# Projections, content products and output products on four column tiles of 32 in a fused attention and gate kernel

## The chip, the cores and the metric

The kernel runs on one core of one Trainium2 chip. The metric is the device time of one execution in microseconds (us). Engine names as in the profile: PE is TensorE (matmuls), PEld its weight loads, DVE is VectorE, ACT is ScalarE, POOL is GpSimd, SP is SyncE, which issues the DMAs.

## The reference

The input `x` has 8 batches of 256 rows of 512 values. It is normalized, goes through a latent attention with 128 heads and through a feed-forward branch, and the two are multiplied and added to `x`. Everything is float32.

```python
xn = layernorm(x)                                            # 8 x 256 x 512
c_q, c_kv = xn @ Wq_down, xn @ Wkv_down                      # latents of 64
q_c = (c_q @ Wq_up).reshape(b, s, 128, 4)                    # content part of the queries
q_r = (xn @ Wq_rope).reshape(b, s, 128, 64)                  # the large projection: 512 x 8192
k_c = (c_kv @ Wk_up).reshape(b, s, 128, 4)
v_c = (c_kv @ Wv_up).reshape(b, s, 128, 4)
k_r = xn @ Wk_rope                                           # one for all heads
scores = (q_c . k_c + q_r . k_r) / sqrt(68)                  # per head, 256 x 256
out = (softmax(scores) @ v_c).reshape(b, s, 512) @ Wo
g = silu(ffn(xn))
result = x + out * g
```

## The kernel before

A first phase of about 260 us normalizes `x`, transposes it, computes the latents and the gate `g` of all rows, and leaves them in DRAM. Its matmuls have their own lines (L364 to L471). The attention follows, in 64 blocks of 16 heads of one batch: `blocks` goes over pairs of batches, within a pair over eight groups of heads, and within a group over the two batches. There is no scheduler: the order of instructions on each engine is the order in the code.

A block has two halves. In each half the loop issues, for TensorE, in this order:

1. `score` twice (tiles `sc`, L613): the content part from `qcm` and `kc`, then two parts from `qr` and `act`. These matmuls use 32 rows of the array each, four beside one another ("32*128" in the profile). They write four banks of PSUM.
2. one `Project` (tiles `q`, L162): a quarter of the large projection of a pair of batches, in seven products by Strassen's scheme, each over two chunks of 128 rows, 256 columns wide. That is 14 matmuls. `first` issues eight of them into four banks, ScalarE takes the four banks out (`take`, L202), `second` issues six more. There are 128 projections; four are made in the first phase and 124 in the main loop, two to a block in the first 62 blocks.
3. in the first half of a block only: every second block the content products `qk` of a coming group (`prepare`, L234 and L235), then the value products `av` of the block before (`weigh`, L657), 64 matmuls with 32 columns of weights, on four column tiles of the array ("128*32"). Block 0 has no `weigh`. After some blocks `values` follows (L261), also on column tiles.
4. in the second half of some blocks: the output products `po` of 128 rows (`finish`, L702), four matmuls with 512 columns.

Meanwhile VectorE finds the maxima of the scores (L626) and transposes the exponentials (L642), ScalarE makes the exponentials (L632) and takes the banks out, GpSimd joins the projection's sums (L207 to L209) and spreads the queries (L246). The weights of the next projections (`w`, `ws`) come by DMA from SP's queue; the sums of `x` (`xs`) come once for each pair of batches, four times in all, into a single buffer.

All banks of PSUM come from one pool of eight (`bank`), each of 128 partitions by 512 values. The matmuls of L162, L234, L235 and L702 fill all 128 partitions of their part of a bank in one instruction ("128*128"); those of L657 fill 32 partitions each:

```python
for k in range(8):
    for r in range(4):
        nc.tensor.matmul(
            av[32 * r : 32 * r + 32, ds(half * P, P)],
            vpad[:, k, r, :],
            pt[r][:, k].rearrange("p q i -> p (q i)"),
```

The functions that the diff touches, and what calls them:

Of the kernel before, what the change touches and what calls it, by code (L numbers as in the profile page):

```python
# [15 lines left out]
P = 128  # L16
B, S, D = 8, 256, 512
NT = B * S
KT = D // P
# [14 lines left out]
def mla_ffn_gate_kernel(  # L34
# [19 lines left out]
    nc = tc.nc  # L54
# [8 lines left out]
    wupq_sb = const.tile([P, 4, P], F32, name="wupq_sb")  # L63
    wupk_sb = const.tile([P, 4, P], F32, name="wupk_sb")
# [30 lines left out]
    def bank(name):  # L95
        return ps_all.tile([P, 512], F32, tag="b", name=name)
# [4 lines left out]
    acts, qks, qcms, valls, vpad_of, qrs = {}, {}, {}, {}, {}, {}  # L101
# [52 lines left out]
    def load_xs(p):  # L154
        if p < B // 2:
            xsums[p] = xsp.tile([P, 7, 2, S], F32, tag="xs", name=f"xs_{p}")
            nc.sync.dma_start(out=xsums[p], in_=xs_d[p])

    def product(bank_, w, x, first):

        for c in range(2):
            nc.tensor.matmul(  # L162
                bank_,
                w[:, c],
                x[:, c],
                start=first and c == 0,
                stop=c == 1,
                skip_group_check=True,
            )

    class Project:

# [20 lines left out]
        def first(self):  # L193

            for i, (w, x) in enumerate(
                ((self.a(0, 0), 0), (self.s[:, 1], 4), (self.s[:, 2], 5), (self.s[:, 0], 3))
            ):
                self.banks.append(bank(f"q{i}_{self.j}")[:, 0:S])
                product(self.banks[i], w, self.x[:, x], True)
# [11 lines left out]
        def second(self):  # L211

            for i, w, x in ((0, self.a(0, 1), 1), (2, self.a(1, 1), 6), (3, self.s[:, 3], 2)):
                product(self.banks[i], w, self.x[:, x], False)
            nc.scalar.copy(self.out(0, 0), self.split(self.banks[0]))
# [14 lines left out]
    def prepare(b, g):  # L230


        qk = bank(f"qk_{b}_{g}")
        nc.tensor.matmul(qk[:, :S], wupq_sb[:, g, :], acts[b][:, 0, :], start=True, stop=True)  # L234
        nc.tensor.matmul(qk[:, S:], wupk_sb[:, g, :], acts[b][:, 0, :], start=True, stop=True)  # L235
        qc = qcp.tile([P, S], F32, tag="qc", name=f"qc_{b}_{g}", bufs=3)
        nc.scalar.copy(qc, qk[:, :S])  # L237
        kc = qcp.tile([P, S], F32, tag="kc", name=f"kc_{b}_{g}", bufs=3)
        nc.scalar.mul(kc, qk[:, S:], QSCALE)
        qks[b, g] = qc, kc  # L240
# [307 lines left out]
    def between(step):  # L548
        if step == 0:
            set_up()  # L550
        elif step == 1:
            load_act(0)
            load_act(1)
            for j in range(2):
                load_rope(j)
        elif step == 2:
            prepare(0, 0)
            prepare(1, 0)
            spread(0)
            values(0)  # L560
            values(1)
            place_values(0)
            sum_w(0)
            sum_w(1)
            load_xs(0)
        elif step == 3:
            for j in range(2):
                Project(j).all()
                load_rope(j + 2)
                sum_w(j + 2)  # L570
        else:
            for j in range(2, 4):
                Project(j).all()
                load_rope(j + 2)
                sum_w(j + 2)
            load_act(2)
            load_act(3)
# [5 lines left out]
    wo_sb = w2p.tile([P, KT, D], F32, name="wo_sb")  # L583
# [11 lines left out]
    scs, nmxs, prs, pts, accs, outT = {}, {}, {}, {}, {}, {}  # L595
# [102 lines left out]
    def finish(b, n):  # L698
        g, xr = gxs.pop((b, n))
        po = bank(f"po_{b}_{n}")  # L700
        for c in range(KT):
            nc.tensor.matmul(  # L702
                po, outT[b][:, c, ds(n * P, P)], wo_sb[:, c, :], start=(c == 0), stop=(c == KT - 1)
            )
        nc.vector.tensor_mul(g, po, g)
        nc.gpsimd.tensor_add(g, g, xr)
        nc.sync.dma_start(out=out[ds(b * S + n * P, P), :], in_=g)
# [6 lines left out]
    for n, (b, sg) in enumerate(blocks):  # L714
        for half in range(2):
# [39 lines left out]
            if half == 0:  # L755
                if n + 2 <= last and blocks[n + 2][1] % 2 == 0:
                    prepare(blocks[n + 2][0], blocks[n + 2][1] // 2)
                if n < last:
                    spread(n + 1)
                if n >= 2 and blocks[n - 2][1] % 2:  # L760
                    normalize(n - 2)
                if n >= 1:
                    weigh(n - 1)
                    place_values(n)
                if (sg == 7 and b % 2) or (sg == 0 and b and b % 2 == 0):
                    if b + 1 < B:
                        values(b + 1)
                if sg == 2 and b >= 2:
                    load_act(b + 2)
            elif n in outs:  # L770
                finish(*outs[n])
    normalize(last - 1)
    load_out(B - 2, 0)
    finish(B - 2, 0)
    load_out(B - 2, 1)
    finish(B - 2, 1)
    load_out(B - 1, 0)
    weigh(last)
# [70 lines left out]
```

## Time and profile before

| what | value |
|---|---|
| median of 3 runs | 2095.45 us (2091.44 to 2098.23) |
| the profiled execution, its own time | 2094.74 us |
| its span | 2093.0 us |
| granted TensorE clock, mean | 0.992 |
| TensorE busy | 2046.5 us (98%) |
| VectorE, ScalarE, GpSimd busy | 1525.3, 1085.1, 719.2 us |
| records of matmuls, and of weight loads | 25536 each |

The span is the time from the first to the last instruction of the profiled execution. Busy time is the time in which at least one instruction of an engine is recorded as running. A record of a matmul has a start that is measured and an end that is modelled, and matmuls overlap, so that the busy time of TensorE and the mean of one instruction say little; the distance of two starts says what one costs. "128*32" stands for the rows and the columns of the array that an instruction uses, "128x256" for partitions by columns of what is streamed through it.

### The profile page before, as it was taken

What the parts mean: (1) busy time and instruction counts of PE and PEld (TensorE: products, weight loads), DVE (VectorE), ACT (ScalarE), POOL (GpSimd) and SP (SyncE); (2) the same over time, 40 slices, a digit from 0 to 9 for tenths busy, and PEclk for the clock granted to TensorE, in tenths of its full rate; (3) what the DMA queues carried; (4) which work ended last, traced back from release to release, by engine and by line L of the source; (5) the groups of instructions that cost most, each with busy time, mean ns of one, the idle gap of its engine ahead of it and who ended that gap; (6) DMA issues with size and microseconds to landing.
All of it is one profiled execution on the core that took longest, in us unless ns stands there. A gap on an engine that the chain in (4) does not pass through costs nothing.

```text
span 2093.0 us, 61071 instructions
## 1 busy us (share of the span) xinstructions
PE 2046.5 (98%) x25536; PEld 1671.2 (80%) x25536; DVE 1525.3 (73%) x2601; ACT 1085.1 (52%) x2989; POOL 719.2 (34%) x1037
## 2 busy tenths in 40 slices
PE   7999999999999999999999999999999999999996
PEld 3334688888888888888888888888888888888883
DVE  5332177878887777878786877788886867788895
ACT  2222265555655555555655545455555544565562
POOL 5335434555452322333233223332223233232321
PEclk9999999999999999999999999999999999999998
DMA  4233322222223132322123222222231232222201
GB/s 161 83 109 117 102 87 82 82 81 73 73 89 121 63 106 84 110 82 78 66 83 118 76 98 94 95 82 82 69 111 68 87 107 87 75 70 82 82 32 52
DMA packets 110262, 183.13 MB, mean 87 GB/s; under 512 B 8154, under 2 KB 80474, under 8 KB 108964
## 3 DMA queue, kind: packets, MB, share of 16 engines
q1 hardware_dynamic: 109988, 179.23, 24.6%
q8 instruction: 203, 3.33, 0.6%
q14 instruction: 71, 0.58, 0.1%
HBM read 145.12 MB, written 34.08 MB: 86 GB/s over the span
## 4 chain that ended last, share of the span: by engine, by line
PE 94%; DVE 2%; DMA 2%; POOL 1%; issue 0%; SPq 0%; ACT 0%; POOLq 0%; ACTq 0%; DVEq 0%
PE q L162 38%; PE sc L613 31%; PE av L657 11%; PE po L702 2%; PE px L428 2%; PE py L429 2%; PE pf L471 1%; PE px L414 1%; DMA xs<-xs_d 1%; DVE pt L642 1%; DVE nmx L626 1%; PE pm L381 1%; PE vps L261 1%; PE qk L234 1%; PE qk L235 1%; PE pp L381 1%
## 5 line engine op out<-in xcount | busy, mean ns | idle before, releaser
L632 ACT ACTIVATE pr<-sc,nmx 128x256 f32<-128x256 f32 x2048 | 818.7, 504 | 488.4 <-DVE nmx L626 486.9
L626 DVE TENSOR_REDUCE nmx<-sc 128x2 f32<-128x512 f32 x1024 | 635.6, 683 | 343.3 <-PE sc L613 311.9
L642 DVE STREAM_TRANSPOSE pt<-pr 128x512 f32<-128x512 f32 x1024 | 635.0, 678 | 0.0
L613 PE MATMUL sc<-act,qr 32*128 32x256 f32 x8192 | 493.8, 375 | 0.2 <-issue 0.2
L162 PE MATMUL q<-xs,ws 128*128 128x256 f32 x2048 | 486.7, 381 | 0.0
L207 POOL TENSOR_TENSOR e<-e,e 128x256 f32<-128x256 f32 x128 | 93.2, 728 | 1089.1 <-ACT e L202 568.9
L613 PEld LDWEIGHTS sc<-act,qr 32*128 32x128 f32 x8192 | 425.1, 185 | 23.1 <-issue 1.0
L162 PEld LDWEIGHTS q<-xs,ws 128*128 128x128 f32 x2048 | 391.4, 191 | 52.5 <-issue 0.2
L162 PE MATMUL q<-xs,w 128*128 128x256 f32 x1536 | 389.7, 390 | 10.3 <-DMA xs<-xs_d 7.5
L162 PEld LDWEIGHTS q<-xs,w 128*128 128x128 f32 x1536 | 292.3, 197 | 80.1 <-ACT pr L632 44.3
L613 PE MATMUL sc<-kc,qcm 32*128 32x256 f32 x4096 | 287.5, 388 | 2.6 <-ACT gs L475 2.5
L613 PEld LDWEIGHTS sc<-kc,qcm 32*128 32x128 f32 x4096 | 201.7, 185 | 53.1 <-issue 22.1
L657 PE MATMUL av<-pt,vpad 128*32 128x128 f32 x8192 | 236.8, 273 | 1.2 <-ACT pr L632 1.2
L657 PEld LDWEIGHTS av<-pt,vpad 128*32 128x32 f32 x8192 | 219.7, 110 | 22.9 <-POOL e L208 8.0
L202 ACT COPY e<-q 128x256 f32<-128x256 f32 x512 | 204.2, 400 | 29.4 <-PE q L162 20.8
L670 ACT ACTIVATE acc<-av,sides_sb 128x256 f32<-128x256 f32 x128 | 53.9, 472 | 242.3 <-PE av L657 242.3
L246 POOL TENSOR_TENSOR qcm<-qc,mask_sb 128x1024 f32<-128x1024 f32 x64 | 122.4, 1912 | 17.0 <-ACT qc L237 17.0
L432 DVE TENSOR_TENSOR hT<-gate,py 128x512 f32<-128x512 f32 (+1 forms) x48 | 32.5, 685 | 110.0 <-PE py L429 109.9
L209 POOL TENSOR_TENSOR qr<-e,e 128x256 f32<-128x256 f32 x128 | 93.8, 732 | 10.0
L208 POOL TENSOR_TENSOR e<-e,e 128x256 f32<-128x256 f32 x128 | 93.5, 730 | 10.0
L219 DVE TENSOR_TENSOR qr<-e,q 128x256 f32<-128x256 f32 x128 | 54.0, 422 | 44.5 <-POOL e L207 34.0
L276 POOL COPY vpad<-vall 32x128 f32<-32x128 f32 x256 | 76.8, 300 | 13.8 <-PE av L657 4.7
(94 smaller groups left out, 1125.4 us busy)
## 6 DMA issues: line engine op xcount, KB each, us to landing
w<-in_w_rope_dram SPq DMA_DIRECT2D x128, 512.0 KB
ws<-sums_d SPq DMA_DIRECT2D x96, 512.0 KB
sums_d<-ws SPq DMA_DIRECT2D x32, 512.0 KB
xs<-xs_d SPq DMA_DIRECT2D x4, 1792.0 KB
xt<-in_x_dram SPq DMA_DIRECT2D x16, 256.0 KB
xs_d<-xt SPq DMA_DIRECT2D x4, 1024.0 KB
gate_d<-gs SPq DMA_DIRECT2D x16, 256.0 KB
g<-gate_d SPq DMA_DIRECT2D x16, 256.0 KB
```

The costliest lines, as they stand in the source:

```text
L162: nc.tensor.matmul(bank_, w[:, c], x[:, c], start=first and c == 0, stop=c == 1, skip_group_check=True,)
L202: nc.scalar.copy(self.e[i], self.banks[i])
L207: nc.gpsimd.tensor_add(m6, m6, m1)
L208: nc.gpsimd.tensor_add(m7, m7, m6)
L209: nc.gpsimd.tensor_add(self.out(1, 1), self.split(m7), self.split(m5))
L246: nc.gpsimd.tensor_mul(qcm, qks[b, sg // 2][0].rearrange("p (q i) -> p q i", i=32).unsqueeze(2).to_broadcast([P, 8, 4, 32]), mask_sb[:, ds ...
L276: nc.gpsimd.tensor_copy(vpad[rows, :, :, 8 * t + 4 * (sg % 2) :][..., :4], valls[b][rows, :, sg])
L613: nc.tensor.matmul(sc[r][:, h, :], lhs.rearrange("p t i -> p (t i)"), rhs, start=(part == 0 and h == 0), stop=(part == 2), skip_group_chec ...
L626: nc.vector.tensor_reduce(nmx[:, r, :], scs[n, f][r], AX.X, ALU.max, negate=True)
L632: nc.scalar.activation(p[:, h, :], scs[n, f][r][:, h, :], AF.Exp, bias=nmxs[n, f][:, r, h : h + 1])
L642: nc.vector.transpose(pts[n, f // 2, r].rearrange("p k q i -> p q k i")[:, ds(2 * (f % 2), 2)], prs.pop((n, f, r)).rearrange("p h (k j) -> ...
L657: nc.tensor.matmul(av[32 * r : 32 * r + 32, ds(half * P, P)], vpad[:, k, r, :], pt[r][:, k].rearrange("p q i -> p (q i)"), start=(k == 0), ...
```

## The change

Each matmul of the projections, of the content products and of the output products is issued as four, which use the same streamed data and 32 columns of the weights each, and write 32 partitions of the same bank each. A new helper `on_columns` issues the four, and `product`, `prepare` and `finish` call it. The order of the work, the tiles, the buffers, the DMAs and the instructions of the other engines stay. The scores (32*128) and the whole first phase, except for its few calls of `prepare` and `Project`, stay as well.

```diff
+    def on_columns(to, w, x, start, stop):
+
+        for t in range(4):
+            tile_ = slice(32 * t, 32 * t + 32)
+            nc.tensor.matmul(to[tile_], w[:, tile_], x, start=start, stop=stop, skip_group_check=True)
+
     def product(bank_, w, x, first):
 
         for c in range(2):
-            nc.tensor.matmul(
-                bank_,
-                w[:, c],
-                x[:, c],
-                start=first and c == 0,
-                stop=c == 1,
-                skip_group_check=True,
-            )
+            on_columns(bank_, w[:, c], x[:, c], first and c == 0, c == 1)
...
         qk = bank(f"qk_{b}_{g}")
-        nc.tensor.matmul(qk[:, :S], wupq_sb[:, g, :], acts[b][:, 0, :], start=True, stop=True)
-        nc.tensor.matmul(qk[:, S:], wupk_sb[:, g, :], acts[b][:, 0, :], start=True, stop=True)
+        on_columns(qk[:, :S], wupq_sb[:, g, :], acts[b][:, 0, :], True, True)
+        on_columns(qk[:, S:], wupk_sb[:, g, :], acts[b][:, 0, :], True, True)
...
         po = bank(f"po_{b}_{n}")
         for c in range(KT):
-            nc.tensor.matmul(
-                po, outT[b][:, c, ds(n * P, P)], wo_sb[:, c, :], start=(c == 0), stop=(c == KT - 1)
-            )
+            on_columns(po, outT[b][:, c, ds(n * P, P)], wo_sb[:, c, :], c == 0, c == KT - 1)
```

## The prediction

> **What bounds the kernel now.** I read the busy time and the slices of the page first, then the chain of waits that ended last, then the instruction groups, and last the timeline of TensorE in the middle of the main loop.
>
> ```profile
> span 2093.0 us, 61071 instructions
> PE 2046.5 (98%) x25536; PEld 1671.2 (80%) x25536; DVE 1525.3 (73%) x2601; ACT 1085.1 (52%) x2989; POOL 719.2 (34%) x1037
> PE   7999999999999999999999999999999999999996
> PEclk9999999999999999999999999999999999999998
> PE 94%; DVE 2%; DMA 2%; POOL 1%; issue 0%; SPq 0%; ACT 0%; POOLq 0%; ACTq 0%; DVEq 0%
> ```
>
> TensorE is busy from slice 2 to the last but one, its clock is granted nearly in full, and 94% of the chain is on it. VectorE, the next engine, has a quarter of the span free. So only the time that TensorE takes for the work can move the end, apart from the first 10 us and a tail of some 40 us.
>
> The groups (line, engine, form, count | busy us, mean ns of one):
>
> ```profile
> L162 PE MATMUL q<-xs,ws 128*128 128x256 f32 x2048 | 486.7, 381 | 0.0
> L162 PEld LDWEIGHTS q<-xs,ws 128*128 128x128 f32 x2048 | 391.4, 191 | 52.5 <-issue 0.2
> L657 PE MATMUL av<-pt,vpad 128*32 128x128 f32 x8192 | 236.8, 273 | 1.2 <-ACT pr L632 1.2
> L657 PEld LDWEIGHTS av<-pt,vpad 128*32 128x32 f32 x8192 | 219.7, 110 | 22.9 <-POOL e L208 8.0
> ```
>
> Two things are to be seen. The counts are twice what the kernel issues (128 projections of 14 matmuls are 1792; this line has 2048 records for `ws` and 1536 for `w`, 3584): a float32 matmul is two passes, each with its own weight load. And a mean of 381 ns is not what a pass costs, because passes overlap. What it costs is read from starts, in the timeline of TensorE (start, us, count):
>
> ```profile
> 1012.65 1.14 PE L162 MATMUL q<-xs,w 128*128 128x256 f32 x4
> 1013.63 2.75 PE L162 MATMUL q<-xs,ws 128*128 128x256 f32 x12
> 1016.22 1.89 PE L162 MATMUL q<-xs,w 128*128 128x256 f32 x8
> 1017.95 1.03 PE L162 MATMUL q<-xs,ws 128*128 128x256 f32 x4
> 1018.90 1.15 PE L613 MATMUL sc<-kc,qcm 32*128 32x256 f32 x16
> ```
>
> Twelve passes from 1013.63 to 1016.22 are 2.59/12 = 0.216 us each. But the first four take 0.98 where 4 x 0.216 = 0.86, and the last four 0.95. Something is lost where the array changes form. The chain of waits gives the same in whole visits (start, us, count):
>
> ```profile
> 1007.33 5.39 PE sc L613 x96
> 1012.72 6.25 PE q L162 x28
> 1018.97 5.39 PE sc L613 x96
> 1024.36 6.25 PE q L162 x28
> 1030.61 0.43 PE qk L234 x2
> 1031.05 0.43 PE qk L235 x2
> 1031.48 3.63 PE av L657 x128
> ```
>
> This repeats to 0.01 us over the loop; almost nothing else is waited for. So the pace within a visit, and what a visit costs beyond its pace, decide.
>
> **What the Trainium skill says.** Three places. (1) "TensorEngine Tiling (Array Packing)", Key Properties: a change of tiling mode drains the TensorE, a change of tile within a mode does not. The trace agrees: the two losses above lie exactly at the changes of form. (2) "TensorE: Matmul & The Clock Gate", Part 1, "Wait — 56ns, not 53.3ns?": back-to-back matmuls start N/2.4 GHz + about 2.5 ns apart. With the trace's 256 columns taken twice, 512/2.4 + 2.5 = 215.8 ns, the 216 above; for the 128 columns of the value products it gives 256/2.4 + 2.5 = 109.2 ns per group of four tiles. (3) The same page, "LDWEIGHTS (loading the stationary operand)": a load lasts as long as its columns at 1.2 GHz, so 107 ns for 128 and 27 ns for 32, 80 less. The trace has 191 and 110 ns, 81 less.
>
> **The price of a visit.** The projections: 28 x 215.8 ns = 6.04 us, against 6.25 measured: **0.206 us** for a visit in the full form (with three digits; the rounded lines say 0.21). The value products: 128 records are 32 groups of four, 32 x 109.2 ns = 3.495 us, against 3.631: **0.136 us** for a visit on column tiles. The difference, 0.07 us, has a reason in (3): after a drain the first weights can't be loaded beside a running pass, and 32 columns are in 80 ns sooner; the last tile starts a little after the first, which takes some of that back.
>
> **The change part by part.**
> (a) Instructions. The 1792 matmuls of the projections, 64 of `qk` and 64 of `po` become four each. In records: 3584 + 128 + 128 = 3840 passes become 15,360, so 11,520 more matmuls and as many loads.
> (b) The pace. A pass of four tiles streams the same 256 columns, so I keep 0.216 us: the value products show four column tiles at once at 109.2 ns for half the columns, with four loads and four matmuls inside that time, twice as dense as the projections will be. The output products stay at 512 columns; the groups of four of that width in the first phase (L443) last 2 x 429 ns plus one visit. So no gain, and in my estimate no loss. What the trace doesn't show is four tiles that stream the *same* data (each of the value products reads a `pt` of its own). Bounds: 0 below, since the columns must be streamed; above, one stagger of tile starts for each pass, some 20 ns (the rival below). I take 0.
> (c) The half of a block with `weigh` (61 times). Before: a full visit of q (and qk), then a visit of av, 0.206 + 0.136 us. After: all on column tiles, one visit, 0.136. Gain 0.206 us, 61 times: 12.6 us.
> (d) The other halves (62, and that of block 0). q is a visit between two scores; it stays one, but on column tiles: 0.206 - 0.136 = 0.07 us, 63 times: 4.4 us. Bounds of this term: 0, if what I took for the form is due to the 128 columns of the value products, and 0.206 x 63 = 13 us if the visit cost all but vanished.
> (e) qk and po lie next to q in the same form before and after; their visits are already counted. In the first phase q and qk stand beside column-tile work on one side and full-form work on the other, so the number of visits stays: 0. In the last 38 us the chain is on VectorE: 0.
> (f) Waits. The first of the four carries the waits of the matmul that it replaces, for the same engines; nothing new is queued. The copies of ScalarE (`e`) wait for the last tile, which starts some 0.02 us after the first: hidden, since TensorE waited only 2.6 us for L202 in the whole span. SP's and POOL's queues and their DMAs are not touched.
> (g) Instruction supply. 51,072 TensorE records now cost at most the 3.33 MB and 203 packets of the instruction queue; 23,040 more make about 1.5 MB, 92 packets. The densest stretch stays that of the value products, 256 records in 3.63 us, and it runs without a gap; a projection visit will have 224 in 6.2 us. Hidden; bounds 0 and, if each new packet were waited for, about 1 us (0.6% of 16 x 2093 us over 203) x 92 = 90 us.
> Does the shorter time reach the end? VectorE waits 312 us for scores, so it follows. The three reloads of `xs` (some 2 to 5 us of TensorE each) stay as they are, because the reload starts at the last product of the pair.
> **Sum:** 12.6 + 4.4 = 17.0 us. The profiled execution took 2094.74 us (span 2093.0); less 17.0 that is 2077.7. It lies 0.7 us under the median shown, so 2078.4 against 2095.45.
>
> **The rivals.**
> *Only the merging pays.* If a visit costs the same in both forms, (d) is 0: 2095.4 - 12.6 = 2083. For it: entry and exit of the scores also cost about 0.2 us together, with loads of 128 columns, so I can't separate width from form; against it: the loads of 81 ns less.
> *The change doesn't do what it says.* If the array drains too where the moving shape goes from 256 to 128 columns, and visits cost the same, 2095. Against it: q to qk to qk runs on at 0.43 us for two passes, across other tiles and buffers, though never across widths.
> *Four streams of the same rows get in each other's way, and it is slower.* Place: each pass of q, qk and po. For it: the case isn't in the trace. Against it: four streams from other tiles run undisturbed. It decides from 17.0 us / 3840 = 4.4 ns per pass on; at the 20 ns stagger the loss is 77 us, less 17: 2095.4 + 60 = 2155.
>
> **How the numbers follow.** The likeliest case (visits merged and shortened, pace kept) has 0.78, its own range 2074 to 2083: run medians scatter by some 3.5 us, and (d) may pay more than I count. Merging alone: 0.08. No effect: 0.05. Slower through the pace or the supply of instructions: 0.09. A measurement of this kernel tells about 0.3%, 6.3 us, from no change. Faster by more than that: 0.78 and most of the 0.08, 0.85; within: 0.06; slower: 0.09. The range goes from 2073 to 2090: the likeliest case, the merging alone, and a pace up to 3 ns a pass worse.
>
> **What the profile after would show.** q in the chain beside `weigh`, with qk and av behind it: from the start of q to the next score 10.54 us for 28 + 4 + 32 groups, instead of 6.16 + 0.96 + 3.63 = 10.74. q between two scores: 6.18 us instead of 6.25. q as 128*32 with 14,336 records and loads of about 110 ns. The scores still 5.39 us. Wrong is the step (b), if the starts within a visit lie more than 0.216 us apart from group to group; wrong is (c), if q, qk and av keep a gap between them; wrong is (g), if "issue" appears as what ended TensorE's waits.

## The result, and the profile after

Four runs of the changed kernel have a median of 2079.24 us (2078.11 to 2081.47), against 2096.09 us for four runs of the kernel before: 16.9 us less by the medians. The ratio is 0.9932 with a 95% interval of 0.9917 to 0.9947, that is 11 to 17 us less, 14 us in the middle. That the two medians differ by almost exactly the 17.0 us forecast is chance: each rests on four runs that scatter by 3 to 7 us. A second set of six runs, beside later experiments, gave 2079.92 us and a ratio of 0.9927 (0.9913 to 0.9942). The profiled execution took 2081.47 us, its span 2079.7 us, 13.3 us less than before. In one experiment below (e11) two of four executions were granted only 0.56 and 0.75 of the TensorE clock throughout, and the ratios leave them out.

The page after, cut to the busy time, the instruction queue and two groups of TensorE:

```profile
span 2079.7 us, 84373 instructions
PE 2030.7 (98%) x37056; PEld 1433.6 (69%) x37056; DVE 1525.4 (73%) x2601; ACT 1083.3 (52%) x2989; POOL 719.7 (35%) x1037
...
q8 instruction: 293, 4.80, 0.9%
...
L163 PE MATMUL q<-xs,ws 128*32 128x256 f32 x8192 | 492.8, 381 | 0.0
...
L163 PEld LDWEIGHTS q<-xs,ws 128*32 128x32 f32 x8192 | 268.0, 111 | 179.2 <-issue 4.3
```

TensorE has 37,056 matmul records, 11,520 more than before, and still bounds the kernel. The busy time of VectorE, ScalarE and GpSimd is within 2 us of what it was. A load lasts 111 ns on average, and the busy time of all loads fell, though there are four times as many in the products that changed. The instruction queue moved 293 packets where it moved 203: 90 more for 23,040 more records of matmuls and loads, so 256 records to a packet. The texts of e8 and e11 call this a piece of the instruction stream.

The pace inside a visit is read from starts, as before (start, us, count):

```profile
1022.04 1.91 PE L163 MATMUL q<-xs,w 128*32 128x256 f32 x32
1023.76 1.05 PE L163 MATMUL q<-xs,ws 128*32 128x256 f32 x16
1024.63 0.61 PE L163 MATMUL qk<-act,wupq_sb 128*32 128x256 f32 x8
```

From 1022.04 to 1024.63 there are 48 records, or 12 groups of four, so 2.59/12 = 0.216 us for a group, the same as for one pass before. Nothing got cheaper inside a visit.

The chain of waits in the middle of the loop (start, us, count):

```profile
1013.24 5.39 PE sc L612 x96
1018.63 6.18 PE q L163 x112
1024.81 0.86 PE qk L163 x16
1025.67 3.49 PE av L656 x128
1029.17 5.39 PE sc L612 x96
1034.56 6.18 PE q L163 x112
1040.74 5.39 PE sc L612 x96
```

A projection between two scores is 6.18 us instead of 6.25. The one beside the value products, with qk and av behind it, is 6.18 + 0.86 + 3.49 = 10.53 us instead of 6.25 + 0.86 + 3.63 = 10.74. The scores stay at 5.39.

What TensorE waited for, out of the table of its waits after (total us, times, longest):

```profile
PE q L163 <- DMA xs<-xs_d: 6.7, 2, 3.4
...
PE q L163 <- ACT pr L631: 2.0, 1, 2.0
...
PE vps L260 <- issue: 1.0, 3, 0.4
...
PE sc L612 <- issue: 0.2, 1, 0.2
```

"issue" means that the trace shows nothing that it waited for. Before, `vps` (the tiles of `values`) and `sc` had 0.2 us of it each. The reloads of `xs` are three: the stop of 2.0 us that the table puts down to ScalarE's `pr` stands at the first of them, where the table of the kernel before names `xs` (7.5 us, three times, 3.0 at most). So the three reloads cost 8.7 us of stops here and 7.5 before.

### The profile page after: what moved, and what is told of

Same layout as the page of the kernel before. It is cut to its first block, busy times and chain, and to the rows that moved or that the text cites. A ratio compares the mean times of both kernels' runs of the same rounds, so it can differ in the third digit from the quotient of the medians.

```text
span 2079.7 us, 84373 instructions
## 1 busy us (share of the span) xinstructions
PE 2030.7 (98%) x37056; PEld 1433.6 (69%) x37056; DVE 1525.4 (73%) x2601; ACT 1083.3 (52%) x2989; POOL 719.7 (35%) x1037
## 4 chain that ended last, share of the span: by engine, by line
PE 93%; DVE 2%; DMA 2%; issue 1%; POOL 1%; ACT 0%; SPq 0%; POOLq 0%; ACTq 0%; DVEq 0%
PE q L163 38%; PE sc L612 32%; PE av L656 10%; PE px L427 2%; PE po L163 2%; PE py L428 2%; PE pf L470 1%; PE qk L163 1%; PE px L413 1%; DMA xs<-xs_d 1%; PE pm L380 1%; PE vps L260 1%; PE pp L380 1%; DVE nmx L625 1%; DVE pt L641 1%
## 5 line engine op out<-in xcount | busy, mean ns | idle before, releaser
L163 PE MATMUL q<-xs,ws 128*32 128x256 f32 x8192 | 492.8, 381 | 0.0
L163 PE MATMUL q<-xs,w 128*32 128x256 f32 x6144 | 384.5, 383 | 12.0 <-DMA xs<-xs_d 6.7
L163 PEld LDWEIGHTS q<-xs,ws 128*32 128x32 f32 x8192 | 268.0, 111 | 179.2 <-issue 4.3
L163 PEld LDWEIGHTS q<-xs,w 128*32 128x32 f32 x6144 | 187.0, 110 | 166.6 <-ACT pr L631 42.0
L656 PEld LDWEIGHTS av<-pt,vpad 128*32 128x32 f32 x8192 | 226.1, 110 | 13.0 <-issue 2.5
L201 ACT COPY e<-q 128x256 f32<-128x256 f32 x512 | 202.8, 397 | 32.7 <-PE q L163 23.8
```

The source lines that it names most:

```text
L163: nc.tensor.matmul(to[tile_], w[:, tile_], x, start=start, stop=stop, skip_group_check=True)
L201: nc.scalar.copy(self.e[i], self.banks[i])
L656: nc.tensor.matmul(av[32 * r : 32 * r + 32, ds(half * P, P)], vpad[:, k, r, :], pt[r][:, k].rearrange("p q i -> p (q i)"), start=(k == 0), ...
```

## The experiments

The theory: every visit of TensorE to one form of the array costs a fixed time beyond its passes (0.206 us full, 0.138 us on column tiles of 32), and visits of one form that follow each other are one visit. The main rival: the passes themselves became cheaper. In e1 to e4 the helper takes a width (`product` passes it on):

```diff
-    def on_columns(to, w, x, start, stop):
+    def on_columns(to, w, x, start, stop, wide=32):
-        for t in range(4):
-            tile_ = slice(32 * t, 32 * t + 32)
+        for t in range(128 // wide):
+            tile_ = slice(wide * t, wide * t + wide)
```

### e1: only the first half of each block

```diff
-                product(self.banks[i], w, self.x[:, x], True)        # second alike
+                product(self.banks[i], w, self.x[:, x], True, 32 if self.j % 2 == 0 else 128)
...
-            on_columns(po, outT[b][:, c, ds(n * P, P)], wo_sb[:, c, :], c == 0, c == KT - 1)
+            on_columns(po, outT[b][:, c, ds(n * P, P)], wo_sb[:, c, :], c == 0, c == KT - 1, 128)
```

> Column tiles only for the projection in the first half of each block (the half that has the value products) and for the content products; the projection of the second half and the output products in the full form. Theory (each visit to the array in one form costs 0.206 us in the full form and 0.138 us on column tiles, and the visits of one form are merged): 61 merged visits save 0.206 us each, so 12.6 us less than before, about 2083.5; in the profile 10.54 us from q over qk and av to the next score, and 6.25 us for q between two scores as before. Rival (the pass itself got cheaper on narrow tiles, 17.0 us / 3840 = 4.4 ns each): half the passes, so 8 to 8.5 us less, and q in the first half 0.12 us shorter by its own pace.

Measured: 2083.78 us against 2094.62 (27 runs of before, shared by e1 to e4); ratio 0.9948 (0.9935 to 0.9961), 8 to 14 us less. The total does not separate the two; the chain does:

```profile
1005.59 6.25 PE q L163 x28
1011.84 5.39 PE sc L612 x96
1017.24 6.18 PE q L163 x112
1023.41 0.86 PE qk L163 x16
1024.28 3.49 PE av L656 x128
```

q with qk and av is 10.53 us where it was 10.74, of which 0.14 us is won in the av behind it and not in a pass of q, and q between scores is back at 6.25. These are the theory's visits, to 0.01 us.

### e2: only the second half of each block

```diff
-                product(self.banks[i], w, self.x[:, x], True)        # second alike
+                product(self.banks[i], w, self.x[:, x], True, 128 if self.j % 2 == 0 else 32)
...
-        on_columns(qk[:, :S], wupq_sb[:, g, :], acts[b][:, 0, :], True, True)      # kc alike
+        on_columns(qk[:, :S], wupq_sb[:, g, :], acts[b][:, 0, :], True, True, 128)
```

> Column tiles only for the projection in the second half of each block, where it stands between two scores, and for the output products; the projection of the first half and the content products in the full form. Theory: nothing is merged, 62 visits cost 0.138 instead of 0.206 us, so 4.2 us less than before; q between two scores 6.18 us, q with qk 7.11 us and av 3.63 us as before. Rival 1 (only merging pays): 0 us, q between two scores 6.25. Rival 2 (a cheaper pass, 4.4 ns each): 8.5 us less.

Measured: 2091.37 us; ratio 0.9983 (0.9975 to 0.9992), 2 to 5 us less. The theory's 4.2 lies inside, the rivals' 0 and 8.5 outside. The chain:

```profile
1014.81 5.39 PE sc L612 x96
1020.20 6.25 PE q L163 x28
1026.45 0.86 PE qk L163 x4
1027.32 3.63 PE av L656 x128
1030.95 5.39 PE sc L612 x96
1036.34 6.18 PE q L163 x112
```

With nothing merged, av is 3.63 us as before; q on column tiles alone saves its 0.07 us.

### e3: one more change of form inside each projection

```diff
             for i, w, x in ((0, self.a(0, 1), 1), ...):
-                product(self.banks[i], w, self.x[:, x], False)
+                product(self.banks[i], w, self.x[:, x], False, 128)
```

> All as after the change, but the second six matmuls of each projection in the full form: one more change of form inside each projection. Theory: each projection has a visit on column tiles (16 passes, 3.45 + 0.138 = 3.59 us) and one in the full form (12 passes, 2.59 + 0.206 = 2.80 us), together 6.39 us against 6.25 before and 6.18 after; with what follows (qk and av, or po, on column tiles again) 136 x 0.138 = 19 us more than before, 36 us more than after the change, about 2115. Rival (a cheaper pass): 16 of 28 passes keep their gain, so some 9 us less than before.

Measured: 2122.69 us; ratio 1.0129 (1.0114 to 1.0144), 24 to 30 us more. The sign refutes the rival: 16 of 28 passes are on column tiles, and the kernel is slower than before. The visits cost what was expected:

```profile
1007.71 6.39 PE q L163 x76
1014.10 1.00 PE qk L163 x16
1015.10 3.49 PE av L656 x128
1018.59 5.91 PE sc L612 x96
```

A projection is 6.39 us, and qk pays for the entry of the next visit (1.00 instead of 0.86). That is 19 us. Of the other 9, some 3 are two more stretches of 3.4 us at half the granted clock than before (see e6); most of the rest are stops ahead of scores or inside them, such as the score of 5.91 us here. TensorE's waits put 1.6 us of these down to "issue"; what the others wait for is not settled.

### e4: two tiles of 64

```diff
-    def on_columns(to, w, x, start, stop, wide=32):
+    def on_columns(to, w, x, start, stop, wide=64):
```

> Projections, content products and output products on two column tiles of 64 in place of four of 32; the value products stay on tiles of 32, so nothing is merged. Theory, with the entry set by the load of the first weights[...]: a visit costs about 0.15 us, q between two scores 6.19 us, q then av 6.19 + 3.63; 125 x 0.055 = 7 us less than before. Rival 1 (any column tiling has the price of the value products, whatever its width): 6.18 us, 8.5 us less. Rival 2 (only tiles of 32 pay): 6.25 us, 0.

Measured: 2086.15 us; ratio 0.9963 (0.9949 to 0.9976), 5 to 11 us less: the total excludes rival 2 only. The chain and, below it, a group of the loads:

```profile
1037.66 6.20 PE q L163 x56
1043.86 5.39 PE sc L612 x96
1049.25 6.20 PE q L163 x56
1055.45 3.63 PE av L656 x128
```

```profile
L163 PEld LDWEIGHTS q<-xs,ws 128*64 128x64 f32 x4096 | 297.5, 137 | 146.4 <-issue 0.9 <-POOL ws L133 0.2
```

The visit costs 6.198 - 6.043 = 0.155 us (the chain rounds it to 6.20), between 0.206 for 128 columns and 0.138 for 32, as its load of 137 ns lies between 191 and 110. Rival 1 is out: the width of the tiles counts, not tiling as such. Narrower tiles are also more tiles, so that the load as the cause fits the three prices, but is not isolated by them. And av is 3.63 again: tiles of 64 and of 32 are two forms, so nothing merges.

### e5: the first phase on column tiles too

```diff
     # over_xn, alike the large products of both gate layers:
-    nc.tensor.matmul(ps, weights[:, c, :], xnT[tb][:, c, :], start=(c == 0), stop=(c == KT - 1))
+    on_columns(ps, weights[:, c, :], xnT[tb][:, c, :], c == 0, c == KT - 1)
```

The small products that open a sum in the gate branch are closed by themselves here (`stop=True`).

> The change, and in the first phase the matmuls of the latents, of the gate branch (the large ones of both layers) on four column tiles as well. Theory: 12 visits of the small second-layer products on column tiles merge with a neighbour (0.2 us each) and 16 more visits get 0.07 us shorter: 3.4 us less than after the change if TensorE sets the pace of the first phase, less where it waits; the first score of the main loop starts at about 254 us instead of 257.1. Rival (visits in the first phase are hidden behind other engines): no difference, 257.

Measured: 2084.43 us (2076.05 to 2089.22) against 2094.95; ratio 0.9948 (0.993 to 0.9967). That is no gain over the change (0.9932, 0.9927), and the intervals overlap. The first score starts at 250.1 us, but in the other kernels above and below, whose first phase keeps the full form there, it starts anywhere from 255.0 to 258.2 us, and in e7 and e9, which have the first phase of e5, at 255.0 and 257.5, so the visits won there are not resolved. What was lost came later: TensorE's stops at `vps` marked "issue" are 2.4 us, in a main loop whose instructions are the same. This led to e8.

### e6: the sums of x in two tiles

```diff
-            xsums[p] = xsp.tile([P, 7, 2, S], F32, tag="xs", name=f"xs_{p}")
-            nc.sync.dma_start(out=xsums[p], in_=xs_d[p])
+            xa = xsp.tile([P, 4, 2, S], F32, tag="xa", name=f"xa_{p}")   # read by first
+            nc.sync.dma_start(out=xa, in_=xs_d[p][:, 0:4])
+            xb = xsp.tile([P, 3, 2, S], F32, tag="xb", name=f"xb_{p}")   # read by second
+            nc.sync.dma_start(out=xb, in_=xs_d[p][:, 4:7])
```

The sums are also stored in another order, so that each tile is one stretch of `xs_d`, and the products take theirs from `xa` or `xb` (left out here).

> The change, and the sums of x (xs) in two tiles, those that the first eight products of a projection read and those that the last six read; the reload of the first can start 2.6 us earlier. In the profile after the change TensorE stands still 2.2, 3.6 and 3.4 us before the first projection of a pair, and the passes that follow are paced at 427 instead of 216 ns for eight passes (1.7 us) each time: 14 us in all. Theory (the wait is the time of the transfer less the 5.4 us of scores beside it): the waits fall below 0.5 us, the slow passes go with them, 12 us less than after the change, about 2067. Rival (the transfer is late because of the queue ahead of it, not because of its start): 3 us or less.

Measured: 2064.51 us; ratio 0.9861 (0.9844 to 0.9878), 14 us below the change by the ratios. After the change, the chain shows the visit behind the stop of 2.0 us:

```profile
644.81 7.94 PE q L163 x112
```

It takes 1.76 us more than 6.18; eight passes at 427 instead of 216 ns are 1.7. The record of the granted clock has the same factor: in this stretch the clock was 0.50 (from and to, us, busy time and instructions of PE, PEld, DVE, ACT and POOL, granted clock, DMA share, GB/s):

```profile
645.40:648.80 3.40, 3.40 (x40) 2.16 (x32) 3.40 (x6) 1.11 (x3) 0.00 (x0) 0.50 0.27 104
```

Such a stretch followed two of the three reloads before the change (stops of 2.3 and 3.0 us, not the one of 2.2) and all three after it. What decides whether one follows is not tested. With xs in two, the same place:

```profile
642.30 6.18 PE q L168 x112
648.48 0.86 PE qk L168 x16
649.34 3.49 PE av L662 x128
```

TensorE no longer waits for xs at all, the granted clock is 1.00 from 642.3 to 648.5 us, and the slow passes are gone with the stops at all three reloads. In the profile after the change these were 8.7 us of stops and three times 1.7 us of slow passes, together the 14 us won. The rival (the queue ahead) is out. With e9 this is the fastest kernel of the case.

### e7: both

> The change with both of the others: the first phase on column tiles and xs in two tiles. If they are independent, the sum of their gains: 3 + 12 = 15 us less than after the change, about 2064.

Measured: 2075.64 us; ratio 0.9911 (0.9894 to 0.9928), 10 us slower than e6 by the ratios. They are not independent. In the profiles most of it lies in the main loop, 1742.9 us against 1733.9 in e6 from the first score to the last projection, though the loop's instructions are the same. The first phase on column tiles has 1984 more records of matmuls and loads, which is 192 more than seven times 256, so the loop stands 192 records further on in the pieces than in e6. In e5 it is the same against the change.

### e8, e9: the same loop further on in the instruction stream

```diff
             ps = bank(f"{name}_{tb}")
+            if tb == 0 and name == "pm":
+                for _ in range(48):          # 16 in e9, on top of e7
+                    nc.tensor.matmul(ps[0:32, 0:32], ident[:, 0:32], ident[:, 0:32],
+                                     start=True, stop=True, skip_group_check=True)
```

> The kernel with xs in two tiles, and 48 matmuls of 32x32 without use ahead of the first latents, 192 records of TensorE and loads, which cost some 3 us at the start. With the first phase on column tiles as well, the instructions of the main loop stayed the same but stood 192 records (of 256 in a fetched piece) further on, and TensorE's stops at the values (vps) after a long stretch of column tiles grew from 1.6 to some 5 us in six places. Theory (the stops are the instruction supply, and depend on where the pieces of the stream end): the stops at vps become about 1 us each, 4 to 6 us in all, as with both; total about 2064.5 + 3 + 4 = 2071. Rival (the stops come from something else in that kernel): they stay at 1.6 us in all, total about 2067.

> The kernel with the first phase on column tiles and xs in two, and 16 matmuls of 32x32 without use ahead of the first latents, 64 records, so that the main loop's instructions stand a whole number of 256 records further on than with xs in two alone. Theory of the supply: the stops at vps shrink to about 1.6 us in all, and 3 to 4 us are won against the same without the 16 (about 2072). Rival: they stay at about 5 us, total 2076 or above.

Measured, against 2095.84 us: e8 2079.16 us, ratio 0.992 (0.9908 to 0.9933), 12 us slower than e6 by the ratios and more than expected. e9 2066.91 us, ratio 0.9862 (0.9849 to 0.9875), 10 us *faster* than e7, though it executes 16 matmuls more. The "issue" stops of TensorE in e6 and then in e8:

```profile
PE vps L266 <- issue: 0.7, 2, 0.5
```

```profile
PE vps L266 <- issue: 2.5, 4, 1.0
PE sc L624 <- issue: 2.4, 3, 1.4
```

Of the 12.1 us by which e8's main loop is longer (1746.0 against 1733.9 us from the first score to the last projection), they are 4.2; the rest are smaller stops ahead of scores and projections, and passes at the slow pace behind a stop.

Eight profiles, those of the change, of e5 to e10 and of e12 below, share the instructions of the main loop, and they fall in two groups. Where the loop stands 192 records further on (e5, e7, e8, e12), the "issue" stops at `vps` are 2.4, 2.6, 2.5 and 4.4 us; where it stands where it did, or a whole number of 256 further on (the change, e10, e6, e9), they are 1.0, 1.4, 0.7 and 0.9 us. The first phase and the tiles of xs differ within each group.

### e11: a whole piece further on

The same with 64 useless matmuls, 256 records.

> The kernel with xs in two, and 64 useless matmuls of 32x32 ahead of the first latents, 256 records in place of 192: a whole piece of the instruction stream. With 192 the time was 2079.2 us against 2064.5 without any, and TensorE's stops marked as issue 4.9 us against 0.7. Theory (the place of the main loop in the pieces of 256 decides): back to about 2065 us, stops marked as issue under 1.5 us. Rival (useless matmuls at the start cost by themselves, or any change of the stream does): 2079 or above.

Measured: 2068.32 and 2071.91 us; ratio 0.9878 (0.9859 to 0.9897), 9 us below e8 by the ratios, though still 3 to 4 us above e6, and above the forecast. More useless work than e8, and faster: the rival is out, and most of e8's loss is undone. How many stops are left in these two is not known.

### e10 and e12: the changed kernel again, and shifted

e12 has the 48 matmuls of e8 in the changed kernel.

> The changed kernel once more, beside these: q between two scores 6.18 us, q to the next score 10.54 us, the stops at vps about 1.5 us in all if they depend on the stream alone and not on the execution; about 2079.

> The changed kernel (xs in one) with 48 useless matmuls, 192 records, ahead of the first latents. Theory: the visits stay at 6.18 and 10.54 us, and the stops at the values and the scores grow by some 5 to 12 us, so 2085 to 2091 instead of 2079. Rival (the changed kernel has enough stops at xs for the supply to catch up): within 3 us of 2079.

Measured: e10 2079.92 us, with the visits at 6.18 us and, by the chain, 6.18 + 0.86 + 3.49 us, and 1.4 us of "issue" at `vps`. e12 2088.69 us, ratio 0.9967 (0.9954 to 0.998), 8 us slower than e10 by the ratios. Its waits:

```profile
PE vps L260 <- issue: 4.4, 4, 1.4
...
PE sc L618 <- issue: 1.7, 4, 0.5
```

and one of the places, in the timeline:

```profile
684.54 1.26 PE L260 MATMUL vps<-wv_sb,act 128*32 128x128 f32 x34
686.50 1.07 PE L260 MATMUL vps<-wv_sb,act 128*32 128x128 f32 x30 [0.71 <-issue]
```

Between 34 and 30 of the 64 matmuls of `vps` TensorE stands still. The 30 read the same two tiles as the 34, and from the 33rd on they write the same bank, so neither data nor a bank was missing. It is the end of the longest stretch on column tiles without a change of form: q, qk if it is due, av and vps, which are 608 or 640 records of matmuls and loads, 384 of them (av and vps) in the last 5.2 us. From the first score to the last projection e12 took 1755.1 us and e10 1750.3; 4.4 of these 4.8 us are "issue" stops at `vps` and `sc`. The two spans differ by 8.9 us; the other 4 lie ahead of the loop and behind it.

## Why the prediction was right, and where not

**The bound and the pace, (a) and (b): right.** The records are those counted, and the starts within a visit stay at 0.216 us from group to group. Four tiles that stream the same columns don't disturb each other here; the slower rival, which needed 4.4 ns a pass, is out. The prediction fitted the pace by counting the columns of a pass twice; its sum rests on the measured 0.216 us, not on a reason for the doubling. In e2, where nothing else changed, the projection is exactly its visit shorter.

**(c), the merged visits: right.** 10.53 us by the rounded lines, 10.54 by the starts, 10.54 forecast. e1 shows this part alone, and e3 that visits put in cost what visits of their form cost: from q to the next score 6.39 + 1.00 + 3.49 = 10.88 us, 0.35 more than after the change, for one visit in the full form and one on column tiles (0.206 + 0.138).

**(d), the shorter visits: right.** 6.18 us as forecast. e2 shows it alone. e4 agrees with the reason that the prediction took from the lengths of loads: 0.206, 0.155 and 0.138 us for loads of 191, 137 and 110 ns. A visit gets cheaper as its first load gets shorter, but not by all of it (68 of 81 ns), as said. That the load is the cause stays argued, since the number of tiles changes with its width.

**(e), (f): right within a microsecond or so.** Nothing new appears among the waits; those of TensorE for ScalarE's copies (L201) grew from 2.6 to 3.3 us. The shorter time reached the end. One reading in (e) was off: the chain is on VectorE in the 38 us from 2025.5 us on, not in the last 38. It cost nothing: from the start of the last projection to the end the kernel took 73.3 us before and 72.8 after.

**(g), the supply of instructions: wrong as "hidden", though inside its bounds.** The packets of the instruction queue came as forecast (203 to 293, 3.33 to 4.80 MB), but "issue" did appear at `vps`, 1.0 us in the profile after and 1.4 us in e10, against 0.2 before. The prediction took the value products' stretch for the densest and looked no further than its length; it did not look at what follows on it, the six `vps`, nor at the projection ahead of it, which was a thin stretch of 56 records of matmuls and loads and is now one of 224. With the stream shifted, the changed kernel loses 8 us (e12), about half of what the change gains, and the kernel with xs in two 12 us (e8). That the supply is the cause is argued from the label, from e5, e7, e8 and e12 (192 records further on, slower) and from e9 and e11 (a whole number of 256 further on, faster). No record shows the wait itself.

**The sum.** The forecast of 17.0 us is the sum of the visits, and for these it holds: between first score and last projection the visits that run without a stop are shorter by 63 x 0.067 and 61 x 0.205 us by their starts, together 16.7. The kernel as a whole got 14 us by the ratio and 13.3 us by the profiled spans; the loop alone went from 1762.3 to 1749.8 us, 12.5 less. In these two profiles the 4.2 us between the visits and the loop are mostly at the reloads of `xs`: 1.2 us more of stops, and 1.7 us for a third stretch at half the granted clock where there had been two. Another 1.3 us are at the six `vps`. The part at the reloads changes from one execution to the next (e10, the same kernel, has two such stretches), so it can't be put down to the change.

**The rivals.** Merging alone and no effect are excluded by e2's interval and by the chain. The slower rival had the wrong mechanism; what could have taken much of the gain away is the place in the instruction stream, which was counted in the same 0.09. That this kernel's loop stood at a good place was luck: the prediction did not ask where it stood.

## What to carry to other kernels

Count a kernel's changes of form on TensorE before its matmuls: each visit to a form cost a fixed time here, less with narrower tiles, and neighbours brought to one form share one visit; the pace stayed at 0.216 us when four tiles did the work of one matmul. But four times the instructions make long dense stretches, and how long TensorE stops in these went with where they lie in the stream; a gain of under a per cent should be measured with the stream shifted once or twice. And look for the rare long wait first: three waits for one buffer, with the slow passes behind them, were worth 14 us, as much as the whole change.

## What the runs showed that was not expected

The time went up and down by 8 to 12 us with the place of unchanged instructions in TensorE's stream: 48 useless matmuls (192 records) at the start cost 12 us between e6 and e8, and 16 useless ones won 10 us between e7 and e9, by the ratios.

A stop of TensorE of 2.0 to 3.4 us can be followed by passes at 427 instead of 216 ns, about eight of them: the visit of 7.94 us above. The granted clock is 0.50 in this stretch of 3.4 us. The stop costs more than its length, and the e6 edit won both.
